# MLP up weights scaled and rounded in one ScalarE operation, lower parts on VectorE

## The chip, the cores and the metric

The kernel runs on one core of a Trainium2 chip. A core has five engines that each work through an instruction queue of their own, in order: TensorE (PE in the profile; its weight loads are PEld), VectorE (DVE), ScalarE (ACT), GpSimd (POOL) and SyncE (SP), which here issues the DMA transfers. The metric is the time of one execution on the device, in microseconds.

## The reference

The input `x` (4 x 1024 x 256) is normalised to `xn`. Two branches read it. One is a 16-head attention with rotary positions ("the head" below). The other is a stack of two layers, each a local attention (8 heads, window 128) followed by a gated MLP; its result goes through SiLU and gates the first branch.

```python
x = L0_attn_x
xn = _layernorm(x, axis=-1)
s = _L0_attn_ref(xn, w_qkv, w_out)
g = _silu(_L0_ffn_ref(xn, ...))      # two layers
return x + s * g

# the MLP of a layer
h = shift_token(x)
h = (h - mu) / jnp.sqrt(var + 1e-05) * lg + lb
h = h @ w1 + b1
a, g = jnp.split(h, 2, axis=-1)
h = a * jax.nn.gelu(g, approximate=False)
x = x + h @ w2 + b2
```

The change touches only how `w1` is made ready. The factor `lg` of the normalisation is folded into the rows of `w1`, and `lb @ w1` is folded into the bias.

## The kernel before

Products that need float32 accuracy are made of three matmuls (`mm3`) over operands that are split in two: an upper part, rounded to the matmul's float32 form (`w1_h`), and a lower part, the difference (`w1_l`). `split` makes such a pair: ScalarE copies and rounds, and VectorE (or the engine that is named) subtracts.

The kernel does not issue its instructions directly. Every call is recorded (`Recorder.record`, line 191) with a price (`price`, line 273) and a due time `nc.vt`. `lay_out` (line 339) then places all recorded operations on a timeline of its own: each engine takes, among the operations whose inputs and buffers are ready by the priced times, the one with the smallest due time. In that model operations of VectorE and GpSimd that touch no PSUM (`locks`) exclude each other. `put` (line 501) issues everything in the order found; because of that, all instructions carry its line, L536, in the profile, and tile names tell them apart. The order on each queue is fixed once written, so a change in what one operation waits for can alter the order of everything behind it.

Two streams are woven together by due times. The head has 64 steps (8 stacks of 8 heads): scores `sc` on TensorE, exponentials `es` on ScalarE, products `acc` on TensorE, and ahead of those a pass `mx` whose maxima `nm` VectorE takes. The layers run in phases 2 to 5: attention 0, MLP 0, attention 1, MLP 1. The head's instructions belong to no phase and fill in everywhere.

`mlp_phase` (line 1276) opens with the weights. `vec` holds `lg` and `lb` for the two halves of the 256 input rows. The raw `w1` (two halves of 128 x 1408) is loaded into `w1st`; 44 one-column matmuls `pb` multiply it by `lb`, and VectorE adds the result to the bias. Then each half is multiplied by `lg` in place on VectorE and split, with the subtraction on GpSimd. After it, `load_split` (line 1052) brings `w2` in two pieces `w2s` (1024 and 512 columns), and in layer 1 `wouts`, each split with GpSimd as well. `w1st`, `w2s`, `wouts` and the first block's `ge` all carry the tag `ge` in a pool with one buffer, so each waits until the one before it has been read for the last time.

Then come eight blocks of 512 rows. For each, `ht` is loaded, normalised on VectorE, transposed (`dT`) and split (`dh`, `dl`); eleven groups `up` multiply it by `w1_h` and `w1_l`; the results go to `ge`, through GELU, and through `w2` (`y`). In layer 1 the output projection of the head (`foT`, `fs`) is part of each block.

Of the kernel before, what the change touches and what calls it, by code (L numbers as in the profile page):

```python
# [13 lines left out]
AF = mybir.ActivationFunctionType  # L14
ALU = mybir.AluOpType
# [532 lines left out]
def f32(ap):  # L548
    return ap.bitcast(F32)
# [30 lines left out]
def fused_kernel(  # L580
# [17 lines left out]
    nc = Recorder(tc)  # L598
# [92 lines left out]
    def split(hi, lo, src, lo_eng=None):  # L691

        nc.scalar.copy(hi, src)
        (lo_eng or nc.vector).tensor_tensor(lo, src, f32(hi), ALU.subtract)
# [581 lines left out]
    def mlp_phase(layer):  # L1276
# [7 lines left out]
        w1_h = wp.tile([P, 2, W1T], F32R, name=f"w1h{layer}")  # L1284
        w1_l = wp.tile([P, 2, W1T], F32R, name=f"w1l{layer}")
        vec = wp.tile([P, 2, 2], F32, name=f"vec{layer}")
# [6 lines left out]
        sts = [st[:, half] for half in range(2)]  # L1293
# [11 lines left out]
        m = 64 + TAIL  # L1305
        nc.vector.tensor_tensor(b1_sb[:m, 10:11], b1_sb[:m, 10:11], pb[:m, 10:11], ALU.add)
        for half in range(2):
            nc.vector.tensor_scalar(sts[half], sts[half], vec[:, 0, half : half + 1], None, ALU.mult)
            split(w1_h[:, half], w1_l[:, half], sts[half], nc.gpsimd)
        w2_h = wp.tile([P, NKT * D], F32R, name=f"w2h{layer}")  # L1310
        w2_l = wp.tile([P, NKT * D], F32R, name=f"w2l{layer}")
        load_split(p1, "ge", w2_h, w2_l, w2[layer], f"w2s{layer}")
# [124 lines left out]
    for layer in range(LAYERS):  # L1437
        attention_phase(layer)
        mlp_phase(layer)
# [91 lines left out]
```

## Time and profile before

| | |
|---|---|
| median of 3 runs | 2186.66 us (2186.58 to 2187.71) |
| profiled execution | 2186.66 us, span 2184.9 us |
| mean granted TensorE clock | 0.985 |
| raw `w1` scaled on VectorE (`w1st<-w1st,vec`, 128x1408) | 4 times, 0.945 us median |
| upper parts on ScalarE (`w1h<-w1st`, 128x1408) | 4 times, 1.368 us median |
| lower parts on GpSimd (`w1l<-w1st,w1h`, 128x1408) | 4 times, 3.197 us median |
| preparation in layer 0: `w1st` issued, `pb`, first `up` | 808.6, 816.7 to 822.7, 850.5 us |
| preparation in layer 1: `w1st` issued, `pb`, first `up` | 1863.6, 1872.9 to 1880.05, 1913.5 us |

"Busy" is the time in which an engine has an instruction in execution; the span is the time from the first to the last instruction of the profiled execution. An engine's idle time counts only where the chain that sets the end runs through it. The granted clock is the share of full speed that TensorE was allowed.

### The profile page before, as it was taken

How to read it: one execution, taken by the hardware profiler on the slowest of the kernel's cores; microseconds unless marked ns; L12 is line 12 of the kernel's file. 1: busy time of each engine (PE TensorE's matmuls, PEld its weight loads, DVE VectorE, ACT ScalarE, POOL GpSimd, SP SyncE). 2: the span in 40 equal slices, each digit the busy share in tenths (PEclk: the TensorE clock that was granted, in tenths of full speed). 3: DMA queues.
4: the chain of work that ended last, by engine and by line, in shares of the span. 5: the costliest groups of instructions: out<-in, count | busy, mean ns of one | idle time of the engine just before them, and what ended most of it. 6: DMA issues, size and time to landing. Idle time of an engine off the chain costs nothing.

```text
span 2184.9 us, 46495 instructions
## 1 busy us (share of the span) xinstructions
PE 2079.8 (95%) x16640; PEld 1379.1 (63%) x16760; DVE 1662.3 (76%) x4008; ACT 1604.4 (73%) x3830; POOL 1101.9 (50%) x1373
## 2 busy tenths in 40 slices
PE   5899999999999999999999999999999999899998
PEld 4356656666676654876665556666567665378787
DVE  6898798898888876576558888888888887765433
ACT  4578878778778767565658878777877888676774
POOL 5346655565666523333127556675657554233424
PEclk8899999999999999999999999999999999999999
DMA  4856655575565452231134534454254344503212
GB/s 128 169 120 163 160 127 123 126 159 111 111 132 127 87 135 75 75 84 60 35 87 112 133 77 102 103 125 100 69 120 105 84 88 89 149 13 94 87 40 83
DMA packets 496255, 227.62 MB, mean 104 GB/s; under 512 B 336788, under 2 KB 479264, under 8 KB 496024
## 3 DMA queue, kind: packets, MB, share of 16 engines
q1 hardware_dynamic: 496024, 224.63, 44.0%
q8 instruction: 133, 2.18, 0.4%
q14 instruction: 98, 0.80, 0.1%
HBM read 111.30 MB, written 49.82 MB: 74 GB/s over the span
## 4 chain that ended last, share of the span: by engine, by line
PE 64%; ACT 15%; DVE 9%; DMA 3%; issue 3%; POOL 3%; SPq 2%; ACTq 0%; POOLq 0%; DVEq 0%
PE up L536 11%; PE acc L536 7%; PE sc L536 7%; PE qkv L536 7%; PE mx L536 6%; PE y L536 6%; ACT sm L536 4%; PE po L536 4%; ACT es L536 3%; PE px L536 3%; PE sb L536 3%; DVE rotb L536 2%; PE pp L536 2%; DVE nm L536 2%; ACT ph L536 2%
## 5 line engine op out<-in xcount | busy, mean ns | idle before, releaser
L536 DVE TENSOR_REDUCE nm<-mx 128x1 f32<-128x512 f32 x1024 | 668.5, 681 | 97.8 <-PE mx L536 88.3
L536 ACT ACTIVATE es<-sc 128x512 f32<-128x512 f32 x1024 | 574.8, 600 | 154.9 <-PE sc L536 134.4
L536 PE MATMUL sc<-sq,sk 128*128 128x512 bf16 x992 | 336.3, 385 | 23.5 <-ACT es L536 17.3
L536 PE MATMUL mx<-sk,sq 128*128 128x512 bf16 x936 | 327.2, 388 | 30.1 <-DVE nm L536 17.1
L536 POOL TENSOR_TENSOR ph<-sm,ph 128x1024 f16<-128x1024 f32 (+1 forms) x128 | 258.7, 2021 | 176.7 <-ACT ph L536 165.9
L536 PE MATMUL qkv<-wqkvh,ht 128*128 128x512 f32 x768 | 300.2, 433 | 1.9 <-ACT sqv L536 0.5
L536 PE MATMUL acc<-es,v 128*32 128x512 f32 x2048 | 276.5, 609 | 1.2 <-issue 0.3
L536 ACT ACTIVATE sm<-sm,nb 128x256 f32<-128x256 f32 (+1 forms) x512 | 247.4, 489 | 4.0
L536 POOL TENSOR_TENSOR qr<-rotb 128x256 f32<-128x256 f32 x256 | 182.9, 733 | 132.5 <-DVE rotb L536 120.5
L536 PEld LDWEIGHTS <-sq 128*128 128x128 bf16 x1024 | 89.7, 99 | 160.1 <-issue 115.6
L536 PEld LDWEIGHTS qkv<-wqkvh,ht 128*128 128x128 f32 x768 | 145.3, 189 | 57.0 <-DVE mxb L536 4.9
L536 PEld LDWEIGHTS <-pht 128*128 128x128 f16 x4800 | 151.5, 98 | 44.5 <-issue 28.9
L536 DVE TENSOR_TENSOR rotb<-qkv,tab 128x1024 f32<-128x1024 f32 x128 | 155.9, 1219 | 24.1 <-ACT sqv L536 9.8
L536 PEld LDWEIGHTS <-sk 128*128 128x128 bf16 x1024 | 89.0, 98 | 133.5 <-issue 93.9
L536 POOL TENSOR_TENSOR hl<-ge,hh 128x512 fp32r<-128x512 f32 x96 | 122.2, 1290 | 94.6 <-ACT hh L536 93.7
L536 PE MATMUL po<-vs,pht 128*128 128x64 bf16 x4800 | 161.6, 193 | 2.4 <-DMA pht<-ph 1.6
L536 PE MATMUL qkv<-wqkvl,ht 128*128 128x512 f32 x384 | 151.1, 393 | 0.0
L536 PE MATMUL up<-dh,w1h 128*128 128x512 f32 (+1 forms) x352 | 150.5, 428 | 0.1
L536 POOL TENSOR_TENSOR sqv<-sqv 128x512 f32<-128x512 f32 (+1 forms) x128 | 129.4, 1011 | 36.4 <-ACT sqv L536 35.0
L536 PE MATMUL up<-dh,w1l 128*128 128x512 f32 (+1 forms) x352 | 139.4, 396 | 0.0
L536 PE MATMUL up<-dl,w1h 128*128 128x512 f32 (+1 forms) x352 | 139.2, 396 | 0.0
L536 POOL MEMSET ge<- 32x512 f32 (+1 forms) x48 | 25.0, 521 | 203.3 <-ACT ge L536 201.4
(272 smaller groups left out, 4814.8 us busy)
## 6 DMA issues: line engine op xcount, KB each, us to landing
xc<-xt_d SPq DMA_DIRECT2D x56, 256.0 KB
qk<-th SPq DMA_DIRECT2D x128, 96.0 KB
xt_d<-nt SPq DMA_DIRECT2D x32, 256.0 KB
ht<-xt_d SPq DMA_DIRECT2D x64, 128.0 KB
tab<-tab SPq DMA_DIRECT2D x64, 128.0 KB
xa<-xr SPq DMA_DIRECT2D x64, 128.0 KB
ht<-xa SPq DMA_DIRECT2D x32, 256.0 KB
xm<-xa SPq DMA_DIRECT2D x16, 512.0 KB
```

The costliest lines, as they stand in the source:

```text
L536: ins = getattr(getattr(nc, engine), method)(*[take(a) for a in args], **{n: take(a) for n, a in kw.items()})
```

## The change

Neither half is scaled in place any more. ScalarE reads the raw half, multiplies by the per-partition factor and writes the rounded upper part in one operation. VectorE then takes (raw half times factor) minus upper part as the lower part, in one `scalar_tensor_tensor`, where GpSimd subtracted before. `w1st` is only read.

```diff
         for half in range(2):
-            nc.vector.tensor_scalar(sts[half], sts[half], vec[:, 0, half : half + 1], None, ALU.mult)
-            split(w1_h[:, half], w1_l[:, half], sts[half], nc.gpsimd)
+            nc.scalar.activation(w1_h[:, half], sts[half], AF.Copy, scale=vec[:, 0, half : half + 1])
+            nc.vector.scalar_tensor_tensor(
+                w1_l[:, half], sts[half], vec[:, 0, half : half + 1], f32(w1_h[:, half]), ALU.mult, ALU.subtract
+            )
```

## Prediction

> **What bounds the kernel now.** I read the page's busy table first.
>
> ```profile
> PE 2079.8 (95%) x16640; PEld 1379.1 (63%) x16760; DVE 1662.3 (76%) x4008; ACT 1604.4 (73%) x3830; POOL 1101.9 (50%) x1373
> ```
>
> TensorE carries the kernel: 105 us of the 2184.9 us span are without a matmul, and a change gains only by removing such gaps or stretches at a low granted clock. So the next view is the table of windows around the two preparations of the MLP weights. Columns: stretch, its length, busy time (and instructions) of PE, PEld, DVE, ACT, POOL, then granted clock, DMA share, GB/s. First layer 0; its bias matmuls `pb` end at 822.7.
>
> ```profile
> 822.70:826.00 3.30, 3.30 (x11) 2.01 (x9) 3.17 (x14) 0.71 (x3) 0.00 (x0) 0.50 0.04 13
> ...
> 828.00:830.00 2.00, 0.74 (x5) 0.48 (x5) 0.84 (x2) 2.00 (x3) 2.00 (x1) 1.00 0.00 0
> 830.00:832.00 2.00, 1.65 (x7) 0.39 (x10) 0.00 (x0) 1.90 (x5) 2.00 (x2) 0.68 0.00 0
> 832.00:834.00 2.00, 2.00 (x9) 0.14 (x4) 0.00 (x0) 0.52 (x1) 2.00 (x1) 0.50 0.00 0
> 834.00:836.00 2.00, 1.42 (x8) 0.39 (x10) 0.00 (x0) 1.68 (x4) 0.03 (x1) 0.96 0.46 59
> ...
> 840.00:845.00 5.00, 4.26 (x23) 1.31 (x21) 4.39 (x20) 4.96 (x13) 3.10 (x3) 1.00 0.53 155
> 845.00:850.50 5.50, 4.72 (x31) 1.62 (x30) 4.13 (x11) 4.78 (x11) 2.58 (x5) 1.00 0.38 101
> ```
>
> PE idles 1.26 + 0.35 us while ACT is full (828 to 832), the clock falls a second time (830 to 834), and 0.58 + 0.74 + 0.78 = 2.1 us more go between 834 and 850.5, where the first `up` matmul starts. Then layer 1, whose `pb` ends at 1880.05 and whose first `up` starts at 1913.5.
>
> ```profile
> 1884.00:1886.00 2.00, 1.74 (x8) 0.40 (x10) 2.00 (x1) 1.77 (x3) 2.00 (x1) 0.64 0.00 0
> 1886.00:1888.00 2.00, 1.51 (x10) 0.29 (x3) 2.00 (x2) 2.00 (x4) 2.00 (x2) 1.00 0.00 0
> 1888.00:1890.00 2.00, 1.71 (x11) 0.29 (x10) 2.00 (x2) 1.67 (x4) 1.88 (x1) 1.00 0.00 0
> ...
> 1909.30:1913.50 4.20, 0.68 (x4) 0.14 (x2) 4.20 (x12) 0.62 (x1) 2.59 (x3) 0.91 0.00 1
> ```
>
> The timeline gives what happens there: start, duration, instruction, and idle time before it with its releaser. Layer 0:
>
> ```profile
> 822.98 0.95 DVE L536 TENSOR_SCALAR w1st<-w1st,vec 128x1408 f32<-128x1408 f32 x1
> ...
> 826.30 1.36 ACT L536 CAST w1h<-w1st 128x1408 fp32r<-128x1408 f32 x1
> ...
> 827.73 6.30 POOL L536 TENSOR_TENSOR w1l<-w1st,w1h 128x1408 fp32r<-128x1408 f32 x2 [14.16 <-ACT w1h L536]
> ...
> 834.06 0.36 SPq L536 DMA_DIRECT2D w2s<-in_w  x1
> ```
>
> The scaling in place must wait until `pb` has read the raw weights; rounding and subtracting follow it; and `w2s`, which uses the same buffer (tag `ge`), is loaded only when the second subtraction has ended at 834.03. The waits of SyncE's queue say the same (total, times, longest):
>
> ```profile
> SPq L536 <- POOL w1l L536: 8.3, 1, 8.3
> ```
>
> In layer 1 VectorE suffers beside the same POOL work, and PE later waits for a maximum:
>
> ```profile
> 1886.66 3.22 POOL L536 TENSOR_TENSOR w1l<-w1st,w1h 128x1408 fp32r<-128x1408 f32 x1
> 1886.77 3.26 DVE L536 TENSOR_SCALAR ht<-ht,mv,mrs_0c 128x256 f32<-128x256 f32 x1
> ...
> 1912.87 1.18 PE L536 MATMUL mx<-sk,sq 128*128 128x512 bf16 x2 [3.52 <-DVE nm L536]
> ```
>
> That `ht` scaling has a median of 0.41 us; beside POOL it took 3.26.
>
> **The change, part by part.** It removes per layer two in-place scalings (DVE, 0.945 us each) and two POOL subtractions (3.2 us each). It keeps two roundings on ACT, now with the factor, and adds two scalar_tensor_tensor on DVE. No DMA is added or moved by the text of it, but the planner rebuilds every queue's order from here on.
>
> *ScalarE's operation.* Plain and activated copies of 128x1024 both take 1.048 us, so 128x1408 stays near 1.37; a per-partition operand costs 0.686 - 0.600 = 0.09 us more (`ge<-up,b` against `es<-sc`, both 128x512). I take 1.37 to 1.46 us.
>
> *VectorE's operation.* Two-input operations take 0.418 us for 256 columns and 0.684 for 512, a slope of 1.04 ns; the scalar_tensor_tensor `ge` takes 0.749 at 512. So 1408 columns give 0.749 + 896 x 0.00104 = 1.68 us. Bounds: 0.945, the present scaling, and 3.2, POOL's pass over the same data. I take 1.7, the slope of the same engine.
>
> *What leaves the path.* Raw weights are now only read, so rounding and lower parts need the load and `vec`, not `pb`. Both halves had landed by 816.7, since `pb` starts then and needs both. `pb` holds PE for 6.0 us in layer 0 and 7.15 in layer 1, in which ACT is busy 1.31 and 1.04 us and DVE 3.59 and 3.02: room for 2.7 to 2.9 us of rounding, and for most of 3.4 us of lower parts. I cost these at nothing on the strength of that cover; the part that comes before `pb` (first half: 1.4 us ACT and 1.7 us DVE, ahead of exponentials and maxima PE needs) costs 0 to 3.1 us per layer if the cover is gone, and I take 0.3, as the planner can put them later.
>
> *Layer 0.* Relief of ACT after `pb`: the 1.26 + 0.35 us of PE idle at the roundings go. The second fall of the clock is worth 2 x 0.32 + 2 x 0.50 = 1.64 us at full speed; between 0 and that I take half, 0.8. `w2s` is released at the end of `pb`, 822.8, instead of 834.03: 11.2 us less in which PE has only the head's work, at the idle rate of 2.1 in 16.5 us (13%): 1.4. Together 3.8.
>
> The Trainium skill, "TensorE: Matmul & The Clock Gate", section "Part 1: The HAM clock gate", says that a busy window of about 3.4 us restores the full clock and an idle one takes it away. The rows here agree on two levels, 0.50 and 1.00; by that rule all of the 1.64 would return, making layer 0 4.6 rather than 3.8.
>
> *Layer 1.* PE idle at the roundings, 0.26 + 0.49 + 0.29 = 1.04, goes. `w2s` moves from 1892.12 to at best 1882.7, behind the last `sq` transfer before it: 9.4 us at the idle rate of 2.04 in 19.3 us (1890 to 1909.3): 1.0. The 3.52 us stall before 1912.87 and the slow 6.5 us after it (clock 0.79, 1.37 us) came from `ht` scalings and maxima piled on DVE, with `ht` stretched beside POOL's `woutl`. Both operations stay; whether they meet depends on the new order. Between 0 and 4.9 I take 1.8. Together 3.8.
>
> The Trainium skill, "SBUF — State Buffer", section "Who interferes with whom", says that a VectorE instruction with two SBUF inputs and a GpSimd instruction reading SBUF shut each other out. It speaks against the new form; POOL has 0.40 us of work or less during either `pb`, so by it the sum would lose 0.4 us per layer at most. No row here shows this new pair.
>
> *Sum.* -3.8 - 3.8 + 2 x 0.3 = -7.0 us. The profiled execution is 2186.66 us (span 2184.9 and 1.76 around it), and this is the median of the three runs too: 2186.66 - 7.0 = 2179.7. What is late next is PE itself: MLP stretches such as 870 to 1000 have 0.96 us idle in 130.
>
> **The rivals.**
>
> *The new order is worse in attention layer 1 (slower).* All queues' orders after about 810 us are recomputed. The 690 us from 1170 to 1860 have 690 - 668.6 = 21.4 us of PE idle, 3.1%. In layer 0 the same sort of work had from 1.9% (400 to 600) to 5.4% (200 to 400: 10.7 of 200). At 5.4% layer 1 loses 15.6 us: 2186.7 - 7.0 + 15.6 = 2195.3. It decides once the rate passes 4.8%, where (7.0 + 4.4)/690 = 1.7 points are lost. For it: the spread of those stretches. Against it: the cause of the reorder is two shifts of some 10 us, and 1.9% is as near: -8.6 us.
>
> *The start of the MLP is held anyway.* The transposes `dT`, or SyncE's queue (in layer 1 an `sq` reload waits 8.3 us for PE `sc` just ahead of `w2s`), keep `up` where it is. Then only ACT's relief remains: 1.6 + 0.8 + 1.04 - 0.6 = 2.8 us, 2183.9. The same no-change result follows if ScalarE's rounding is laid behind `pb` in the queue after all, so that the change doesn't do what it says.
>
> **How the numbers follow.** A measurement of this kernel tells from no change about 0.2%, 4.4 us. Forecast (2179.7, own range 2173 to 2182): 0.52. Held start: 0.20. Worse order: 0.28. So faster 0.52, same 0.20, slower 0.28. The range goes from 2172 (all of the clock and stall terms, 0.8 + 3.1 us more than taken, and some of the better order) to 2196, just past the worse order.
>
> **What would show it.** Right: four ACT operations `w1h` starting before or during `pb`, near 1.4 us; four DVE `w1l` near 1.7; no POOL `w1l`; `w2s` issued within 3 us of the end of `pb`; first `up` near 840 and 1904; PE idle down by about 7 us in the two stretches. Wrong: `w1h` waiting on the load with `es` queued behind it; `up` still 28 us after `pb`; or those gains present and PE idle from 1170 to 1860 above 26 us.

## The result, and the profile after

The changed kernel takes 2175.48 us (median of 4 runs, 2175.05 to 2178.46) against 2187.18 us (4 runs): a ratio of 0.9946, 95% interval 0.9934 to 0.9958, or 11.7 us faster. The profiled execution was the slowest of the four, 2178.46 us with a span of 2176.7, so a comparison of the two profiles shows 8.2 of the 11.7 us.

In the page's busy table GpSimd has 12.9 us less, and VectorE and ScalarE have about as much as before:

```profile
PE 2085.6 (96%) x16760; PEld 1376.1 (63%) x16760; DVE 1658.9 (76%) x4008; ACT 1604.4 (74%) x3830; POOL 1089.0 (50%) x1369
```

The profile before lists 16640 matmuls for 16760 weight loads, this one 16760 for 16760: 120 matmul records are missing there, so the 105 us without a matmul that the prediction read off are somewhat too many.

The timeline of layer 0 in the changed kernel (start, duration, instruction, idle time before it and its releaser); `pb` runs from 818.07 to 823.4:

```profile
815.35 1.48 ACT L536 ACTIVATE w1h<-w1st,vec 128x1408 fp32r<-128x1408 f32 x1
...
816.86 1.69 DVE L536 SCALAR_TENSOR_TENSOR w1l<-w1st,vec,w1h 128x1408 fp32r<-128x1408 f32 x1 [0.15 <-ACT w1h L536]
...
818.78 1.47 ACT L536 ACTIVATE w1h<-w1st,vec 128x1408 fp32r<-128x1408 f32 x1
...
820.29 1.69 DVE L536 SCALAR_TENSOR_TENSOR w1l<-w1st,vec,w1h 128x1408 fp32r<-128x1408 f32 x1 [0.55 <-ACT w1h L536]
...
825.34 0.36 SPq L536 DMA_DIRECT2D w2s<-in_w  x1
...
837.50 1.04 ACT L536 CAST w2h<-w2s 128x1024 fp32r<-128x1024 f32 x1
```

Both parts lie before or beside the bias matmuls, and `w2s` is issued 1.9 us after them. But its rounding `w2h` stands at 837.50, 12.2 us after the issue, where the kernel before had 7.2 (834.06 to 841.24).

The windows after `pb` in the changed kernel (stretch, length, busy time and instructions of PE, PEld, DVE, ACT, POOL, granted clock, DMA share, GB/s), layer 0 and then layer 1:

```profile
823.40:828.00 4.60, 4.60 (x19) 2.31 (x17) 4.57 (x26) 1.97 (x6) 0.00 (x0) 0.50 0.41 115
828.00:832.00 4.00, 4.00 (x29) 1.45 (x22) 2.40 (x8) 2.98 (x7) 0.00 (x0) 0.85 0.36 115
832.00:836.00 4.00, 3.91 (x26) 1.62 (x24) 3.66 (x16) 3.36 (x12) 1.22 (x3) 1.00 0.43 126
836.00:840.00 4.00, 3.42 (x23) 1.51 (x22) 2.20 (x7) 4.00 (x8) 1.39 (x1) 1.00 0.00 0
840.00:848.10 8.10, 7.27 (x41) 2.70 (x39) 8.10 (x28) 6.80 (x17) 3.22 (x4) 1.00 0.63 172
```

```profile
1876.50:1884.00 7.50, 7.50 (x40) 3.13 (x38) 6.36 (x25) 4.16 (x11) 0.00 (x0) 0.73 0.37 96
1884.00:1890.00 6.00, 5.69 (x35) 1.82 (x31) 6.00 (x22) 4.80 (x13) 0.00 (x0) 1.00 0.35 102
1890.00:1900.00 10.00, 8.09 (x42) 3.08 (x45) 9.35 (x28) 7.71 (x17) 3.15 (x3) 1.00 0.53 137
1900.00:1910.00 10.00, 7.81 (x47) 2.35 (x39) 9.94 (x35) 7.37 (x18) 2.58 (x2) 1.00 0.10 27
```

From 828 to 836 in layer 0, VectorE was busy 0.84 us before and PE 5.81 of the 8 us; now VectorE works for 6.06 us of it and PE for 7.91. The second fall of the clock (830.74 to 834.15 before) is gone. What held VectorE is in its waits, first before (822 to 851), then after the change (total, times, longest):

```profile
DVE dl L536 <- ACT dh L536: 11.3, 2, 9.9
```

```profile
DVE dl L536 <- ACT dh L536: 1.6, 1, 1.6
```

Before, VectorE's queue had `dl` at its head from 828.84 to 838.78, because `dT` stood late in TensorE's order (837.0, though its input `ht` was scaled by 827.05); no maxima could be taken meanwhile, and in the 16 us after `pb` PE ran one `mx` matmul. After the change `dT` runs at 829.45, and PE ran four.

Single executions wander, so kernels are compared below by stretches between fixed points of each one's profile. "Layer 0" runs from the issue of layer 0's `w1st` to that of attention 1's first weights (`wqs`), "attention 1" from there to layer 1's `w1st`, "layer 1" to the start of the last `up` matmul, "tail" to the end. All in us.

| kernel | start | layer 0 | attention 1 | layer 1 | tail |
|---|---|---|---|---|---|
| before | 808.5 | 330.8 | 724.3 | 297.1 | 24.2 |
| changed | 810.0 | 325.8 | 725.0 | 290.5 | 25.3 |
| layer0_only | 811.0 | 326.0 | 724.8 | 296.2 | 24.1 |
| layer1_only | 809.2 | 329.8 | 724.7 | 288.9 | 25.3 |
| wait_kept | 811.7 | 325.8 | 725.4 | 288.9 | 34.3 |
| lower_on_dve | 811.0 | 329.9 | 724.3 | 293.3 | 32.5 |
| act_alone | 805.3 | 327.5 | 724.3 | 296.4 | 34.2 |
| w2_due_after | 809.3 | 324.8 | 724.6 | 288.8 | 25.0 |
| hop_before | 809.7 | 330.8 | 724.3 | 293.0 | 25.0 |
| hop_after | 803.1 | 324.4 | 724.6 | 288.9 | 25.3 |
| fx2_after | 809.3 | 326.0 | 725.9 | 292.9 | 24.2 |
| fx2_wait_kept | 810.3 | 325.9 | 724.9 | 292.6 | 24.4 |
| fx2_lower_on_dve | 811.7 | 328.4 | 724.8 | 291.8 | 28.6 |
| fx2_act_alone | 808.9 | 327.5 | 724.4 | 295.4 | 28.6 |

Between before and changed, layer 0 lost 5.0 us and layer 1 lost 6.6; the tail gave 1.1 back, attention 1 gave 0.8, and the start, which the change doesn't touch, 1.5.

A layer's time is lost in two ways: PE is idle, or it runs at a granted clock of 0.50 (half of each such stretch counts as lost). In layer 0 the idle time fell from 7.0 to 2.8 us (with the missing records in the first figure) and the loss at low clock from 5.1 to 3.4. In layer 1, up to the last `up`, they fell from 8.7 to 5.9 and from 6.8 to 3.4.

The lengths also hold one thing that is not the edit's doing: `pb` takes 4.9 to 7.15 us, by where a fall of the clock meets it (last section). Without `pb`, layer 0 is 318.9 to 320.5 us in the seven kernels with the new form there and 323.3 to 325.2 in the three with the old. Layer 1 without `pb` is 289.9 before, 284.3 changed, and 284.0 in layer1_only, wait_kept and hop_after; but 286.2 in hop_before, 288.1 in fx2_after and 285.5 in fx2_wait_kept. Layer 0's gain is steady; layer 1's depends on the order.

The runs below come from three chips: layer0_only, layer1_only, wait_kept and lower_on_dve from one, act_alone, w2_due_after and the two hop kernels from a second, the four fx2 kernels from a third. Before ran beside each group, and each ratio is to those executions (medians 2186.57, 2184.86 and 2187.86 us).

### The profile page after: what moved, and what is told of

The parts are those of the page before. It is cut to its first block, busy times and chain, and to the rows that moved or that the text cites. A ratio compares the mean times of both kernels' runs of the same rounds, so it can differ in the third digit from the quotient of the medians.

```text
span 2176.7 us, 46620 instructions
## 1 busy us (share of the span) xinstructions
PE 2085.6 (96%) x16760; PEld 1376.1 (63%) x16760; DVE 1658.9 (76%) x4008; ACT 1604.4 (74%) x3830; POOL 1089.0 (50%) x1369
## 4 chain that ended last, share of the span: by engine, by line
PE 64%; ACT 16%; DVE 9%; DMA 3%; issue 3%; POOL 2%; SPq 1%; ACTq 0%; POOLq 0%; DVEq 0%
PE up L536 11%; PE sc L536 7%; PE acc L536 7%; PE qkv L536 7%; PE mx L536 6%; PE y L536 6%; ACT sm L536 5%; PE po L536 5%; ACT es L536 3%; PE px L536 3%; PE sb L536 3%; DVE rotb L536 2%; DVE nm L536 2%; PE pp L536 2%; ACT ph L536 2%
## 5 line engine op out<-in xcount | busy, mean ns | idle before, releaser
L536 PE MATMUL mx<-sk,sq 128*128 128x512 bf16 x1024 | 352.6, 387 | 22.1 <-DVE nm L536 15.6
L536 PE MATMUL sc<-sq,sk 128*128 128x512 bf16 x1024 | 343.7, 384 | 19.2 <-ACT es L536 15.8
L536 ACT ACTIVATE sqv<-qkv 128x512 f32<-128x512 f32 x128 | 76.5, 597 | 70.5 <-DVE rotb L536 57.1
```

What stands on the lines that cost most here:

```text
L536: ins = getattr(getattr(nc, engine), method)(*[take(a) for a in args], **{n: take(a) for n, a in kw.items()})
```

## Experiments

### One layer at a time

```diff
         for half in range(2):
+            if layer == 0:        # layer1_only: layer == 1
+                ...               # the new form
+            else:
+                ...               # the old form
```

> The new form in layer 0's preparation only; layer 1 keeps the old one. Theory A (cover: rounding and lower parts leave the stretch behind the bias matmuls, so TensorE idles less and runs less at a low clock there): 4 to 6 us faster than before, about 2182, since the two profiles differ by 5.0 us from layer 0's w1 load to the start of attention 1. Theory B (the gain is the luck of the rewritten order): anything from 8 us faster to 5 us slower, and the two single-layer kernels don't add up to 11.7 us.

> The new form in layer 1's preparation only, so the order up to 1860 us is that of the kernel before. Theory A: 5 to 7 us faster than before, about 2181, with TensorE idle and clock loss between the end of the bias matmuls and the first up matmul down by about 3 us and the rest seen as a shorter MLP stretch after it. Theory B: no fixed relation to the 5.4 us that the profiles differ by from layer 1's w1 load to the end; within 2 us of before is as likely.

layer0_only: 2182.58 us, ratio 0.9981 (0.9972 to 0.9990). layer1_only: 2180.35 us, ratio 0.9977 (0.9968 to 0.9986). Of 2186.57 us these are 4.2 and 5.0 us; with the change's 0.9946 both together are worth 11.8. The sum of the parts is 9.2, within what the three intervals allow. In the table each shortens its own layer by 4.9 and 8.2 us, the other one by about 1. Of the 8.2 us 2.3 are `pb` at a higher clock (4.9 us for 7.15); without it layer1_only gains 6.0. So both layers gain, in the stretch that was touched, and within the intervals the parts add up, as theory A had it.

### The wait kept

The factor is passed through an operation that reads the bias result, so that rounding and lower part wait for `pb` again.

```diff
+        lg = wp.tile([P, 2], F32, name=f"lg{layer}")
+        nc.vector.scalar_tensor_tensor(lg, b1_sb[:, 0:2], 0.0, vec[:, 0, :], ALU.mult, ALU.add)
         for half in range(2):
-            nc.scalar.activation(w1_h[:, half], sts[half], AF.Copy, scale=vec[:, 0, half : half + 1])
+            nc.scalar.activation(w1_h[:, half], sts[half], AF.Copy, scale=lg[:, half : half + 1])
             ...
```

> Both layers in the new form, but the factor is copied by a small VectorE operation that reads the bias result, so ScalarE's rounding again has to wait for the bias matmuls. Theory A (the cover of the bias matmuls carries the gain): at least half of the gain is lost, 2181 to 2187. Rival C (what counts is that GpSimd's 6.4 us and VectorE's stall beside it are gone): the gain stays, 2175 to 2179.

2185.36 us, ratio 0.9994 (0.9984 to 1.0004): by its time the gain is gone, as theory A said. The profile contradicts that. Its timeline in layer 0, where `pb` ends at 826.8, has all four operations on the path again:

```profile
827.31 2.83 ACT L536 ACTIVATE w1h<-w1st,lg 128x1408 fp32r<-128x1408 f32 x2
...
829.08 3.27 DVE L536 SCALAR_TENSOR_TENSOR w1l<-w1st,lg,w1h 128x1408 fp32r<-128x1408 f32 x2
...
832.38 0.37 SPq L536 DMA_DIRECT2D w2s<-in_w  x1
```

Yet both layers are as short as in the changed kernel (325.8 and, without `pb`, 284.0 for 284.3), and the loss is all in the tail: 34.3 us against 25.3. Its chain of waits near the end shows why (start, duration, what):

```profile
2170.60 0.74 POOL fx L536
2171.34 0.02 issue
2171.35 3.99 DMA out<-fx
2175.34 0.02 issue
2175.36 3.79 DMA fx<-in_x
...
2179.31 0.72 POOL fx L536
```

The last block's `fx` shares one buffer with the block before it, whose store comes only at 2171.35. In the changed kernel that store is issued at 2157.64 and the load at 2160.57, under the last matmuls. The last piece of the head's output (`o<-oa`) was issued at 2129.76 there and at 2153.32 here: the rewritten order had put the head's last step behind the MLP's last blocks.

### The subtraction alone on VectorE, and ScalarE's part alone

lower_on_dve keeps the old order of scaling and rounding:

```diff
-            split(w1_h[:, half], w1_l[:, half], sts[half], nc.gpsimd)
+            split(w1_h[:, half], w1_l[:, half], sts[half])
```

> The old in-place scaling and rounding are kept, and only the subtraction goes from GpSimd to VectorE. Rival C: nearly all of the gain, 2175 to 2179. Theory A: less than half of it, 2182 to 2187, since scaling, 2.7 us of rounding and now 3 us of subtraction stand behind the bias matmuls.

act_alone takes the change's ScalarE operation and leaves the rest:

```diff
+            nc.scalar.activation(w1_h[:, half], sts[half], AF.Copy, scale=vec[:, 0, half : half + 1])
             nc.vector.tensor_scalar(sts[half], sts[half], vec[:, 0, half : half + 1], None, ALU.mult)
-            split(w1_h[:, half], w1_l[:, half], sts[half], nc.gpsimd)
+            nc.gpsimd.tensor_tensor(w1_l[:, half], sts[half], f32(w1_h[:, half]), ALU.subtract)
```

> ScalarE scales and rounds the raw half in one operation, as in the change; but VectorE still scales the half in place afterwards (behind the bias matmuls) and GpSimd still subtracts. Theory A, with ScalarE's relief as its main part: 3 to 6 us faster than before, 2181 to 2184. Theory A with the lower part as the main one (VectorE beside GpSimd, and the reused buffer): less than 2 us faster, 2185 or more.

lower_on_dve: 2190.45 us, ratio 1.0018 (1.0009 to 1.0027). act_alone: 2190.63 us, ratio 1.0030 (1.0019 to 1.0041). Both are slower than before, by 3.9 and 6.6 us, and both have the long tail (32.5 and 34.2). lower_on_dve lies outside both ranges that were expected of it; act_alone lies in the second of its two. Up to the tail they are 4.8 and 4.1 us shorter than before over layer 0 and layer 1 together. Without `pb` lower_on_dve's layers are 0.4 and 2.4 us shorter; act_alone's layer 0 is 3.5 us shorter and its layer 1 is 1.6 us longer.

In act_alone ScalarE has rounded both halves by 815.5, before `pb` ends at 819.6, and yet PE idles 0.80 us and 0.66 us in these two stretches. VectorE is the full engine in the first; in the second it comes to a stand, and its queue has `dl` at its head for 3.6 us, up to 834.56:

```profile
825.00:829.00 4.00, 3.20 (x18) 1.04 (x18) 4.00 (x4) 3.28 (x7) 3.33 (x1) 1.00 0.00 0
829.00:833.00 4.00, 3.34 (x21) 0.62 (x20) 1.92 (x7) 3.23 (x7) 0.00 (x0) 1.00 0.49 133
```

Its timeline shows the in-place scaling, 0.95 us by itself, stretched beside GpSimd:

```profile
820.93 3.17 POOL L536 TENSOR_TENSOR w1l<-w1st,w1h 128x1408 fp32r<-128x1408 f32 x1 [10.61 <-issue]
...
821.57 3.29 DVE L536 TENSOR_SCALAR w1st<-w1st,vec 128x1408 f32<-128x1408 f32 x1
```

PE's idle time between `pb` and the first `up` in layer 0: 3.71 us before, 3.85 here, 2.73 in lower_on_dve, 2.61 in wait_kept, 1.50 in the changed kernel. `dT` stands 14.5, 13.7, 11.9, 7.1 and 6.0 us behind the end of `pb` in them.

### The same four without the fx tie

```diff
-            xt = p1.tile([P, 4, D], F32, tag="fx", name=f"fx{n}")
+            xt = p2.tile([P, 4, D], F32, tag="fx", name=f"fx{n}")
```

> The changed kernel with two buffers for fx, the last rows of the end's sum, so that the load of the last block's fx need not wait for the store of the block before it. Its tail (last up matmul to the end) had 25.3 us with the load hidden: 0 to 3 us faster than the changed kernel, 2172 to 2176. It is the yardstick for the other three.

> The wait_kept kernel with the same two fx buffers. Theory D (waiting for the bias matmuls costs the preparation nothing; wait_kept lost its gain only in a 34.3 us tail, where a store and a load of fx stand one behind the other): 6 to 9 us faster than wait_kept, within 3 us of fx2_after, 2174 to 2179. Theory A (the cover of the bias matmuls carries the gain): it stays 2182 or more.

> The lower_on_dve kernel with two fx buffers. Theory D: its tail of 32.5 us shrinks by 5 to 8 us and what is left is the part of the preparation that moving the subtraction alone gives, 4 to 6 us faster than before: 2180 to 2183. If the in-place scaling were all that counted: 2185 or more.

> The act_alone kernel with two fx buffers. Theory D: its tail of 34.3 us shrinks by 6 to 9 us, and the preparation keeps the 4 us that its profile shows up to the last up matmul: 2181 to 2184. If ScalarE's part alone gave the whole gain: 2174 to 2177.

| kernel | median us | ratio to before (95%) |
|---|---|---|
| fx2_after | 2181.99 | 0.9974 (0.9964 to 0.9985) |
| fx2_wait_kept | 2179.70 | 0.9962 (0.9949 to 0.9974) |
| fx2_lower_on_dve | 2187.52 | 1.0000 (0.9991 to 1.0009) |
| fx2_act_alone | 2187.48 | 0.9999 (0.9990 to 1.0008) |

Before is 2187.86 us here. Against its own yardstick the kept wait costs nothing: fx2_wait_kept and fx2_after have the same layer 0 (325.9, 326.0) and tail (24.4, 24.2), and overlapping intervals; layer 1 is 292.6 and 292.9, or 285.5 and 288.1 without `pb`. PE's idle time before layer 0's first `up` repeats that of their twins (1.58, 2.61, 2.79 and 3.85 us in the order of the table). Theory D's main point holds, though fx2_wait_kept is 0.7 us above its range. Three expectations missed. fx2_after is slower than the changed kernel, not faster: the second buffer rewrote the order in MLP 1, layer 1 went from 290.5 to 292.9, and the tail had little to give (24.2). And the two half changes come out even with before, 4.5 and 3.5 us above the upper end of what theory D gave them: their tails stayed at 28.6. By its time fx2_lower_on_dve agrees with its rival, the in-place scaling as all that counts; by its profile, with layers 2.5 and 5.3 us shorter than before, it doesn't. The kernel before with two `fx` buffers was not run, so what the second buffer's new order does to the old form is open.

### Another order of the same work

```diff
-HOP = 50.0
+HOP = 52.0
```

> The kernel before, with the planner's allowance between engines 52 instead of 50 ns: the same work in another order, to see what a rewritten order alone does. Theory B (luck of the order): differences of 5 us and more are common, so this one is off by several us. Theory A: within 3 us of before, 2184 to 2190.

> The changed kernel with the same 52 ns. Theory A: 8 to 12 us faster than the kernel before in its 52 ns form. Theory B: the difference between the two 52 ns forms has no relation to 11.7 us.

hop_before: 2180.35 us, ratio 0.9981 (0.9972 to 0.9989), 4 us faster with not one operation changed. hop_after: 2174.89 us, ratio 0.9956 (0.9944 to 0.9969). Before is 2184.86 us here, so the two 52 ns forms differ by 5.5 us. Both expectations of theory A missed: hop_before is several us off, as theory B had it, and the difference is not 8 to 12. What the change is worth thus depends on the order it is put into, 5.5 us here and 11.7 in the order it was made for. The table puts the whole of hop_before's gain in layer 1 (293.0 for 297.1). There the 3.52 us stall that the prediction showed has shrunk, by the waits of PE between 1880 and 1915:

```profile
PE mx L536 <- DVE nm L536: 1.5, 1, 1.5
```

One `ht` scaling beside GpSimd still took 3.43 us in it. Layer 0 is as long as before (330.8), and in hop_after it is 324.4, as in the other kernels with the new form.

### The planner told when w2 lands

```diff
             length = moved + 900.0 - at - op.cost
+            if op.bufs[0].name.startswith("w2s") or (len(op.bufs) > 1 and op.bufs[1].name.startswith("w2s")):
+                length = 1800.0 + op.bytes / RATE
```

> The changed kernel, with the planner told that a w2 piece lands 1.8 us plus its bytes at 200 GB/s after its issue, instead of behind all transfers issued before it. Its plan then puts the first up matmul 8.4 us earlier in layer 0 and some 5 us earlier in layer 1. If an earlier MLP start is worth the idle rate that the prediction used (10 to 13% of the time moved): 1 to 2 us faster than the changed kernel, 2173.5 to 2174.5. If the head's work only changes places with the MLP's: within 1 us of it. If ScalarE then waits in its queue for a load that isn't there: 2 us or more slower.

2173.54 us, ratio 0.9949 (0.9936 to 0.9963): not to be told from the changed kernel's 0.9946. The first `up` now starts 16.3 us after `pb` in layer 0 (839.5) instead of 24.7, and 29.0 instead of 33.5 in layer 1. Layer 0 has 324.8 us for 325.8, but hop_after has 324.4 with its `up` 23.4 us after `pb`: an MLP that starts 8.4 us earlier is worth 1 us or less, and the runs don't tell it from nothing.

## Why the prediction was right, point by point

- **Direction and size.** 7.0 us were forecast, 11.7 came, inside the range (2172 to 2196) and at its fast end. In part this is luck: terms of the sum did not come about as forecast, and others, of the clock and of the order, came out larger. PE's idle time between `pb` and `up` fell by 4.4 us in the two layers together, not by 7.
- **Prices of the operations.** Right: 1.470 us on ScalarE for 1.37 to 1.46 taken, 1.685 on VectorE for 1.7, neither stretched. The per-partition factor costs 1.470 - 1.368 = 0.10 us, for which the prediction had 0.09.
- **What leaves the path.** Right in the trace, wrong in weight. All eight operations lie before or beside `pb`, the cover that the prediction named. But the cover carries no gain in time: with the wait kept, the same operations stand behind `pb`, PE idles 1.1 us more before `up`, and both layers stay as short.
- **Layer 0, ScalarE's relief (1.6 us of the sum).** The weakest step. Before, PE's longest wait did stand behind the second rounding (the 1.11 us at the end of the second line are the idle time before it):

```profile
828.32 1.37 ACT L536 CAST w1h<-w1st 128x1408 fp32r<-128x1408 f32 x1
...
830.24 1.64 PE L536 MATMUL sc<-sq,sk 128*128 128x512 bf16 x3 [1.11 <-ACT es L536]
```

  act_alone frees ScalarE, and this wait is gone; but PE idles as much in all (3.85 for 3.71 us), in shorter waits for exponentials. What it lacked was other work to do: VectorE stood, so there were hardly any maxima to go on with. The window showed this too: VectorE was busy 0.84 us in 828 to 830 and not at all until 836. The relief pays once VectorE is free: 2.61 us with the wait kept, 1.50 without it.
- **Layer 0, the clock (0.8 us).** Right in kind, half in size: the second fall, 3.41 us at 0.50, is gone whole, which is worth 1.7. The first is as long as before, 6.83 us (822.35 to 829.17). The Trainium skill, "TensorE: Matmul & The Clock Gate", section "Part 1: The HAM clock gate", has a busy window of about 3.4 us for the return of the full clock. The traces agree with the step, since 6.83 is twice 3.41, but not with the condition: PE had been busy without a gap since `pb` began at 818.07, and the clock still fell at 822.35.
- **Earlier release of the buffer (1.4 and 1.0 us).** `w2s` did move to 1.9 and 2.3 us behind `pb`. That the MLP would start as much earlier was wrong: 848.1 and 1910.0 instead of near 840 and 1904. SyncE's transfer was early, but ScalarE's `w2h` came only 12.2 and 13.1 us after it, since the planner's model queues a load behind all those issued before it. Telling it otherwise brought `up` to 839.5 and 1902.6, for 1 us or less in layer 0. So the movement was not there, and the rate of 13% (8.4 us x 0.13 = 1.1) is neither shown nor refuted.
- **The rival of a held start.** Its mechanism came true, in layer 1 wholly: `up` stands 33.5 us behind `pb` there for 33.4 before, and 24.7 for 27.8 in layer 0. Its price (2183.9) did not: the layers got shorter all the same, because PE did more of the head's work in that time (in layer 1 it was busy 29.0 us of it for 26.9).
- **Layer 1's stall (1.8 us).** Under-sized. In the changed kernel PE's longest wait for a maximum in that stretch is 0.9 us and the sum of such waits 2.6, for 3.5 before; the fall of the clock at 1912.76, 1.7 us lost, is gone. Together that is 2.6 us. Another 1.7 us of layer 1's gain is chance: the fall around `pb` lasted 6.83 us for 10.24. And hop_before gains 4.0 us in layer 1 by order alone (3.7 without `pb`), so of layer 1's 6.6 us a part of about that size may depend on the order rather than on the change. The runs don't separate it further.
- **The rival of a worse order.** Its mechanism is real, its place was wrong. Attention 1 has 724.3 to 725.9 us in all fourteen kernels. A rewritten order costs in the tail, 24 to 34 us, and in layer 1; in the tail wait_kept, lower_on_dve and act_alone lost all that they had gained.
- **What gives layer 0's 5 us.** Seven kernels with the new form, the wait kept or not, have 324.4 to 326.0, three with the old 329.8 to 330.8. Moving the subtraction alone gives 1.0 to 2.5 against before, hardly more than the spread; ScalarE's part alone gives 3.3 and 3.4 in its two kernels, 2.9 of it behind the first `up`. The whole comes only with both: no work on GpSimd, and no in-place scaling between `pb` and the lower part. That VectorE stood because the planner lets VectorE and GpSimd work on SBUF exclude each other, and so laid `dT` late, fits its code and the times of `dT`, but no run varied that rule.

## What to carry to other kernels

When PE idles beside a full engine, check first which queue has an instruction waiting at its head; the full engine may only be what is left to run. Where a program lays out all orders by a model, a change rewrites everything behind it, so compare stretches of the profile, look where the clock falls in each, and run the same work in a second order (here 2 ns in one allowance, worth 4 us) before a small gain or loss is put down to an edit. An earlier transfer helps only if the instruction that uses it is moved too.

## What was not expected of the hardware

The stretch before layer 0's `w1st`, in the kernels other than the 52 ns ones (their order there is that of before), took from 805.3 to 811.7 us in single executions. Part of that may be the chip: one had 809.2 to 811.7, another 808.9 to 811.7, the third 805.3 and 809.3.

The 44 matmuls of `pb` took 4.9 us where the clock was full throughout and up to 7.15 us where it was granted at 0.66 on average (layer 1: 4.9 us in wait_kept, 7.15 in fx2_wait_kept). The clock's changes in the traces account for it. It is 1.00 or 0.50, and within a trace every two changes lie a whole multiple of 3.41 us apart. In layer 0 before:

```profile
820.50:827.33 6.83, 6.83 (x30) 4.41 (x29) 4.53 (x19) 2.66 (x7) 0.00 (x0) 0.50 0.43 114
827.33:830.74 3.41, 1.80 (x11) 0.69 (x8) 1.51 (x6) 3.23 (x6) 3.01 (x1) 1.00 0.10 29
830.74:834.15 3.41, 3.41 (x12) 0.49 (x12) 0.00 (x0) 1.68 (x3) 3.29 (x2) 0.50 0.00 0
```

In all 28 preparations of the fourteen traces the clock falls to 0.50 between 2.3 and 5.5 us after `pb` begins, a spread of about one such step, although PE shows no gap in `pb`. The sooner it falls, the longer `pb` takes: 7.15 us where it fell after 2.3 us, 5.9 after 3.7, 4.9 where it fell as `pb` ended or later. That fits a clock that can change only at fixed points 3.41 us apart: how much of `pb` runs at 0.50 then goes by where it starts between two of them, and with that up to 2.2 us of a layer's length. Why these matmuls bring the clock down is not shown.
